# Four transformer blocks on one core: aside weight work packed into fewer pieces, output rounding ahead of its turns, one context group's norm on DVE

## The chip, the cores and the metric

The kernel runs on one core of a Trainium2 chip. The metric is the time of one execution on the device in microseconds (us); the times below are medians over runs, and one further execution was taken with the profiler on. The engines are called PE (matmul), PEld (its weight loads), DVE (vector), ACT (scalar), POOL (GpSimd) and SP (which issues most DMAs here).

## The reference

Four cross-attention blocks follow one another on x of 4 x 1024 x 288, with a context of 4 x 64 x 288 and 16 heads of 18. Blocks 0 and 3 are alike: self-attention, cross-attention and a feed-forward net, all with activations rounded to 8-bit levels per token and weights to 8-bit levels per output row:

```python
def quant_act(x):
    s = jnp.max(jnp.abs(x), axis=-1, keepdims=True) / 127.0 + 1e-08
    q = jnp.clip(_ste_round(x / s), -127.0, 127.0)
    return (q, s, jnp.sum(q, axis=-1, keepdims=True))
...
h = layer_norm(x, ln1_g, ln1_b, 1e-06)          # self-attention
q8, s, sm = quant_act(h)
q, k, v = (quant_linear(q8, s, sm, w, b) for w, b in ...)
a8, sa, sma = quant_act(attn(q, k, v))
x = x + quant_linear(a8, sa, sma, wo1, bo1)
h = layer_norm(x, ln2_g, ln2_b, 1e-05)          # cross-attention
q = quant_linear(*quant_act(h), wq2, bq2)
k, v = cond @ wk2.T + bk2, cond @ wv2.T + bv2
x = x + quant_linear(*quant_act(attn(q, k, v, mask)), wo2, bo2)
h = layer_norm(x, ln3_g, ln3_b, 1e-05)          # feed-forward
h = gelu(quant_linear(*quant_act(h), wfc1, bfc1))
return x + quant_linear(*quant_act(h), wfc2, bfc2)
```

Block 1 is an attention to two parts of the context, block 2 a fake-quantised self- and cross-attention with a gated feed-forward; the change touches no instruction of theirs except through `level_pieces`, which block 2 also draws on to prepare block 3's self-attention weights.

## The kernel before

x lies in SBUF as 32 tiles of 128 tokens x 288. `quant_net` runs blocks 0 and 3 in two stages.

**Self-attention (`quant_self`).** For each batch b of 4, head group g of 4 (four heads in one 128-row tile), half of the queries qh of 2 and key tile kt of 8 there is one step: four score matmuls (L2042), two exponentials on ACT (L2052), the four weighing matmuls of the step before (L1998), and then one call of `step()`. `weigh` copies its sum to `oT` on DVE after eight steps (L2009); one step later `turn_heads` transposes it (L1953) and divides by the row sums (L1959, L1960). `step()` hands out one piece of the work that lies beside: first from the list `side` in order, and only if `side` is empty from the generator `spare`. `side` holds `operands` (queries and keys of the next group, 4 pieces), `levels` (norm and rounding of the next batch, 12), `values` (8), `output` (rounding of the attention's result, its turns and the product with `wo` into x, 7 pieces per half batch) and, in the last batch, `early` (12: the norm and turn of the first context group). A piece ends at a `yield`.

`spare` is `ctx_aside` and then `ff_aside`: it checks the mask, makes levels of the weights `wq2`, `wo2`, `wfc1` and `wfc2` (`level_pieces`: a load, row extrema, rounding of 96 x 384 parts on DVE at L1605 to L1611, three transposes on PE at L1621, a copy at L1632 and, for the feed-forward, a store), and projects the context to keys (L1686, L1695, L1706, L1710) and values (L1731). `ctx_aside` has the tag `kv` with one buffer for masks, keys and values; POOL clears it ahead of each use (L1681, L1724). Several of its pieces hold nothing, or only a load or a memset. After the last step come `turn_heads()`, `run(spare)` (all that is left of `spare`) and what is left of `side`.

In `output`, one piece rounds a pair of tiles (`round_levels`, L1436 to L1444 on DVE); the next piece rounds the second pair and turns the first (`turn_levels`: transposes L1456, copy L1459).

**Context and feed-forward (`ctx_stage`, `ff_stage`, in block 0 also block 1's `vip_aside` and `vip_tokens`).** `run_stages` is a planner: generators yield the cost of each piece ("d" DVE, "a" ACT, "g" POOL, "p" PE) and the planner picks which one goes on. Context goes in groups of four tiles; the first (tiles 0 to 3) has been prepared by `early`, the others begin with the norm (`norm_apply`: ACT at L1423, then a product and a sum on POOL at L1426 and L1427), row maximum L1324, scale L1326, scaling L1333, turn L1350. Each group's head loop projects the queries (L2261, product with the scales L2269 on DVE), scores (L2277), exponentials (L2280), weighs (L2288, L2296), turns (L2304) and divides (L2307, L2308). POOL adds the bias of `wo` (L1784).

The instructions are written in this order, but the framework orders them again for each engine when the program is built, by what it takes to be ready.

Of the kernel before, what the change touches and what calls it, by code (L numbers as in the profile page):

```python
# [36 lines left out]
P = 128  # L37
# [4 lines left out]
HP = 32  # L42
# [9 lines left out]
EXP, GELU, SIDE = "exp", "gelu", "side"  # L52
CB = (C + N_TERMS) // NC3
# [1125 lines left out]
class Fast(Net):  # L1179
# [250 lines left out]
    def round_levels(self, h, tag):  # L1430


        nc = self.nc
        _, m, n = h.shape
        sc = self.sm.tile([P, m], F32, tag=f"sc{tag}", name="sc", bufs=10)
        nc.vector.tensor_reduce(sc, h, AX.X, ALU.max, apply_absolute_value=True)  # L1436
        nc.vector.tensor_scalar(sc, sc, 1.0 / 127.0, 1e-8, ALU.mult, ALU.add)
        rs = self.stat([P, m], f"rs{tag}")
        nc.vector.reciprocal(rs, sc)
        q = self.wk.tile([P, m, n], BF16, tag=f"q{tag}", name="q")  # L1440
        for j in range(m):
            t = h[:, j, :]
            nc.vector.tensor_scalar(t, t, rs[:, j : j + 1], MAGIC, ALU.mult, ALU.add)
            nc.vector.tensor_scalar(q[:, j, :], t, MAGIC, None, ALU.subtract)  # L1444
        return q, sc
# [100 lines left out]
    def level_pieces(self, np_, wd, n_in, width, p, put, sw, bias=None):  # L1546
# [24 lines left out]
        yield  # L1571
# [74 lines left out]
    def ctx_aside(self, w, ctxT, mask, cw, np_):  # L1646
# [8 lines left out]
        for b in range(B):  # L1655
            m = np_.tile([P, NTB * T], F32, tag="kv", name="msk")
            nc.sync.dma_start(
                m.rearrange("p (t k) -> p t k", k=T), mask[b].rearrange("(t p) k -> p t k", p=P)
            )
            yield  # L1660
            yield
            self.watch_range(0.0, 0.0, m, "mext")
# [10 lines left out]
        for g in range(NG):  # L1673
# [5 lines left out]
            kg = np_.tile([P, NTB * T], F32, tag="kv", name="kg")  # L1679
            kg = kg.rearrange("p (b k) -> p b k", b=B)  # L1680
            nc.gpsimd.memset(kg, 0.0)  # L1681
            yield
            yield
# [18 lines left out]
            for pr in range(2):  # L1702
# [10 lines left out]
                yield  # L1713
# [3 lines left out]
        wv = np_.tile([P, 1152], F32, tag="wn", name="wn", bufs=3)  # L1717
        wv = wv[:CK, : NC3 * C].rearrange("p (c o) -> p c o", c=NC3)
        nc.sync.dma_start(wv, w["wv2"].rearrange("(c p) o -> p c o", p=CK))
        yield  # L1720
        for b in range(B):
            vb = np_.tile([P, NTB * T], F32, tag="kv", name="vb")
            vb = vb.rearrange("p (j r d) -> p j r d", r=2, d=HP)
            nc.gpsimd.memset(vb, 0.0)  # L1724
            yield
# [71 lines left out]
    def quant_self(self, L, w, beside, ready, early):  # L1797
# [5 lines left out]
        with ExitStack() as es:  # L1803
# [126 lines left out]
            def output(b, hf):  # L1930
                a = state[b]["a"][hf]
                now = None
                for j in range(0, 4 + 2, 2):
                    ahead = None
                    if j < 4:
                        ahead = self.round_levels(a[:, j : j + 2, :], "o")
                    if now:
                        q, sc = now
                        aT = self.wk.tile([CK, NC3, 2 * P], BF16, tag="qTo", name="aT", bufs=1)
                        self.turn_levels(q, CK, aT)  # L1940
                    yield
                    if now:
                        for n in range(2):
                            t = b * NTB + hf * 4 + j - 2 + n
                            self.level_residual(aT, sc, wo, t, n, wo["b"])
                            yield
                    now = ahead
# [27 lines left out]

            def step(n=1):
                while side and n:
                    if next(side[0], side) is side:
                        side.pop(0)
                    else:  # L1980
                        n -= 1
                if n:
                    next(spare, None)
# [220 lines left out]
    def ctx_stage(self, cw, g2, b2, pool, nb, made):  # L2204
# [16 lines left out]
        def tokens(b, hf):  # L2221
# [8 lines left out]
            else:  # L2230
                h = self.wk.tile([P, 4, C], F32, tag="h", name="h", bufs=nb)
                for j in range(4):
                    self.norm_apply(h[:, j, :], t0 + j, stats[b], g2, b2)
                    if j % 2:
                        yield "a1.1&g3.2", 0 if j == 1 else None, SIDE
# [1374 lines left out]
```

## Time and profile before

| what | value |
|---|---|
| median of 3 runs | 4927.91 us (4926.48 to 4930.47) |
| profiled execution, whole | 4935.42 us |
| its span, first to last instruction | 4933.7 us |
| mean granted PE clock | 0.849 |
| busy: PE, DVE, ACT, POOL | 4260.1, 2997.3, 3071.3, 1273.6 us |
| last attention matmul (L1998) to first context matmul (L2261), block 0 | 806.2 to 830.1 us |
| the same, block 3 | 4483.0 to 4501.2 us |

Busy times are over the whole span and mix stages with different limits, so the work is read by stretches of time. A wait is listed as who waited for whom, with sum, number and longest in us. In a line of the timeline, the first number is the start in us from the first instruction, the second the duration, and the square bracket at the end says how long the engine sat idle before it and what ended that.

### The profile page before, as it was taken

What the parts mean: (1) busy time and instruction counts of PE and PEld (TensorE: products, weight loads), DVE (VectorE), ACT (ScalarE), POOL (GpSimd) and SP (SyncE); (2) the same over time, 40 slices, a digit from 0 to 9 for tenths busy, and PEclk for the clock granted to TensorE, in tenths of its full rate; (3) what the DMA queues carried; (4) which work ended last, traced back from release to release, by engine and by line L of the source; (5) the groups of instructions that cost most, each with busy time, mean ns of one, the idle gap of its engine ahead of it and who ended that gap; (6) DMA issues with size and microseconds to landing.
All of it is one profiled execution on the core that took longest, in us unless ns stands there. A gap on an engine that the chain in (4) does not pass through costs nothing. (4 is left out here: it accounts for less than half of the span.)

```text
span 4933.7 us, 63765 instructions
## 1 busy us (share of the span) xinstructions
PE 4260.1 (86%) x23291; PEld 1717.8 (35%) x23291; DVE 2997.3 (61%) x6691; ACT 3071.3 (62%) x4355; POOL 1273.6 (26%) x1910
## 2 busy tenths in 40 slices
PE   4999998878998979997888873899998999997776
PEld 2233323445565411110233331455443233322343
DVE  8454336755654589999787878333234444436775
ACT  3776675664753279998888853212114776675796
POOL 2001002543222476410112224111111000004664
PEclk9999998889999955555697875899998999998888
DMA  3000003100001221000000022001000000001000
GB/s 84 4 4 12 11 9 85 41 31 7 13 13 58 108 63 33 26 6 0 23 27 25 22 94 71 30 9 34 1 3 16 3 4 12 11 20 43 12 17 21
DMA packets 137701, 135.99 MB, mean 28 GB/s; under 512 B 69276, under 2 KB 114972, under 8 KB 135712
## 3 DMA queue, kind: packets, MB, share of 16 engines
q1 hardware_dynamic: 136176, 128.13, 8.7%
q0 software_dynamic: 1200, 3.69, 0.3%
q8 instruction: 185, 3.03, 0.3%
q14 instruction: 140, 1.15, 0.1%
HBM read 79.92 MB, written 43.47 MB: 25 GB/s over the span
## 5 line engine op out<-in xcount | busy, mean ns | idle before, releaser
L2052 ACT ACTIVATE e<-ps 128x1024 f32<-128x1024 f32 x1024 | 992.6, 1021 | 388.2 <-PE ps L2042 377.7
L2042 PE MATMUL ps<-qT,kT 32*128 32x512 f32 x4096 | 630.4, 647 | 5.8 <-DVE sext L1971 5.8
L3076 DVE TENSOR_REDUCE top<-e 128x2 f32<-128x2048 f32 x256 | 563.5, 2275 | 13.9 <-ACT e L3069 13.7
L1998 PE MATMUL ps<-e,v 128*32 128x512 f32 x4096 | 554.7, 613 | 5.2 <-DVE oT L2009 5.2
L3445 PE MATMUL ps<-qk 32*128 32x512 bf16 x1024 | 499.6, 604 | 40.7 <-ACT e L3069 38.9
L3494 ACT ACTIVATE e<-ps 128x1024 f32<-128x1024 f32 x512 | 484.4, 1054 | 79.4 <-PE ps L3485 60.8
L3069 ACT ACTIVATE e<-ps 128x1024 f32<-128x1024 f32 x512 | 520.1, 1152 | 6.7 <-PE ps L3445 3.3
L3497 DVE TENSOR_SCALAR eb<-e 128x2048 bf16<-128x2048 f32 x256 | 321.7, 1260 | 49.2 <-ACT e L3494 46.8
L1780 POOL TENSOR_TENSOR x<-x,y 128x288 f32<-128x288 f32 x192 | 152.7, 804 | 705.9 <-DVE y L1779 416.7
L3485 PE MATMUL ps<-qk,kz 64*128 64x512 bf16 x1024 | 230.1, 446 | 42.3 <-ACT e L3494 38.4
L2042 PEld LDWEIGHTS ps<-qT,kT 32*128 32x128 f32 x4096 | 189.7, 185 | 209.5 <-issue 123.3
L2512 PE MATMUL psf<-hT,w 128*128 128x512 f32 x576 | 257.9, 600 | 0.6 <-ACT hT L2504 0.6
L1426 POOL TENSOR_TENSOR h<-h,g 128x288 f32<-128x288 f32 x168 | 136.5, 814 | 434.1 <-ACT h L1423 424.5
L1998 PEld LDWEIGHTS ps<-e,v 128*32 128x32 f32 x4096 | 81.3, 108 | 399.3 <-issue 348.4
L3445 PEld LDWEIGHTS <-qk 32*128 32x128 bf16 x1024 | 53.1, 99 | 464.8 <-issue 463.9
L3394 ACT ACTIVATE gl<-psf,bf 128x512 f32<-128x512 f32 x72 | 46.0, 684 | 270.0 <-PE psf L2516 265.7
L1355 ACT COPY qT<-ps 128x640 bf16<-128x640 bf16 (+3 forms) x252 | 149.7, 640 | 81.3 <-PE ps L1350 81.1
L1897 POOL TENSOR_TENSOR v<-y,wv1b 128x288 f32<-128x288 f32 x64 | 51.5, 811 | 524.2 <-DVE y L1894 524.2
L3398 DVE SCALAR_TENSOR_TENSOR u<-psf,bf,gl 128x512 f32<-128x512 f32 x72 | 51.1, 746 | 213.6 <-ACT gl L3394 213.6
L1350 PE MATMUL ps<-idb,q 128*128 128x128 bf16 (+2 forms) x1128 | 108.0, 240 | 78.5 <-ACT q L1334 47.1
L277 PEld LDWEIGHTS <-qT 98*128 98x128 bf16 (+2 forms) x1344 | 134.2, 104 | 118.0 <-issue 48.2
L3069 ACT ACTIVATION_READ_ACCUMULATOR e<-ps 128x1 f32 x512 | 172.4, 337 | 0.0
(507 smaller groups left out, 7776.6 us busy)
## 6 DMA issues: line engine op xcount, KB each, us to landing
raw<-y SPq DMA_DIRECT2D x32, 432.0 KB
in<-raw SPq DMA_DIRECT2D x30, 432.0 KB
kz<-qk SPq DMA_DIRECT2D x128, 64.0 KB
wn<-in_L_wfc SPq DMA_DIRECT2D x12, 432.0 KB
x<-in_x SPq DMA_DIRECT2D x4, 1152.0 KB
vvo<-vt SPq DMA_DIRECT2D x16, 288.0 KB
vo<-vvo SPq DMA_DIRECT2D x4, 1152.0 KB
rawq<-y SPq DMA_DIRECT2D x32, 144.0 KB
```

Of the source, the lines that this page charges most:

```text
L1355: nc.scalar.copy(qT[:, c0 : c0 + r, j0 * P : (j0 + per) * P].rearrange("p c (a t) -> p a c t", a=per), ps[:width, : per * r * P].rearrange ...
L1780: nc.gpsimd.tensor_tensor(self.x[:, t, :], self.x[:, t, :], y, ALU.add)
L1998: nc.tensor.matmul(acc[i * HP : (i + 1) * HP, :], lhsT=st["v"][:, kt, h * (D + 1) : h * (D + 1) + HP], rhs=es_[i // 2][:, i % 2, :], start ...
L2042: nc.tensor.matmul(pss[i // 2][:, i % 2, :], lhsT=self.row_tile(kT, i)[:, kt * P : (kt + 1) * P], rhs=self.row_tile(qT, i)[:, qh * 512 : ( ...
L2052: nc.scalar.activation(e, ps, AF.Exp, scale=SCALE)
L2512: nc.tensor.matmul(o, lhsT=lhs(i)[:, c, :], rhs=rhs(i)[:, c, :], start=(c == 0), stop=False)
L3069: nc.scalar.activation(e[:, j, :].rearrange("p (a n) -> p a n", a=2), sc, AF.Exp, scale=rstep, accum_out=sums[:, t, h0 + j : h0 + j + 1],)
L3076: nc.vector.tensor_reduce(top[:, t, h0 : h0 + 2], e, AX.X, ALU.max)
L3445: self.last = self.nc.tensor.matmul(ps[:, c, :], lhsT=self.row_tile(qT, i)[:, g, qt * P : (qt + 1) * P], rhs=self.row_tile(kT, i)[:, g, c ...
L3485: nc.tensor.matmul(pss[i][:, n, :], lhsT=kz[rows, i, kt * P : (kt + 1) * P], rhs=qT[rows, g, qh * 512 : (qh + 1) * 512], start=True, stop= ...
L3494: nc.scalar.activation(e[:, 2 * n : 2 * n + 2, :], ps, AF.Exp, scale=step)
L3497: nc.vector.tensor_scalar(eb, e, MAGIC, MAGIC, ALU.add, ALU.subtract)
```

## The change

- `ctx_aside` yields less often. Pieces that held only a load, a memset or nothing are joined with others: masks, keys and values are fetched or cleared one or two pieces ahead, with two `kv` buffers in place of one, and the two halves of `kb` and the store of the keys become one piece. It has 33 pieces where it had 54.
- The first `yield` after a fetch gives the value IDLE. When the next piece of `spare` follows an IDLE, `step()` lets it go along with a piece of `side`.
- `output` rounds both pairs in its first two pieces, and turns and multiplies them in the six after. `round_levels` uses one tag `qr` for the levels of input and output, where each had its own.
- The norm of the second context group (tiles 4 to 7) is done by `norm_dve` (L1412, L1415, L1416, all on DVE), with the planner's cost "d2.4" per two tiles.

```diff
--- before.py
+++ after.py
@@ -50,6 +50,7 @@
 
 N_TERMS = 6
 EXP, GELU, SIDE = "exp", "gelu", "side"
+IDLE = "idle"
 CB = (C + N_TERMS) // NC3
 
 
@@ -1437,7 +1438,7 @@
         nc.vector.tensor_scalar(sc, sc, 1.0 / 127.0, 1e-8, ALU.mult, ALU.add)
         rs = self.stat([P, m], f"rs{tag}")
         nc.vector.reciprocal(rs, sc)
-        q = self.wk.tile([P, m, n], BF16, tag=f"q{tag}", name="q")
+        q = self.wk.tile([P, m, n], BF16, tag="qr", name="q")
         for j in range(m):
             t = h[:, j, :]
             nc.vector.tensor_scalar(t, t, rs[:, j : j + 1], MAGIC, ALU.mult, ALU.add)
@@ -1568,7 +1569,7 @@
             return m, wn
 
         loaded = [load(c0) for c0 in range(0, oc, per)[:2]]
-        yield
+        yield IDLE
         yield
         for c0 in range(0, oc, per):
             m, wn = loaded.pop(0)
@@ -1652,14 +1653,25 @@
         nc.sync.dma_start(bk, w["bk2"])
         bv = self.load_bc(np_, w["bv2"], C, "bv2")
         ctx = self.load_ctx(np_, ctxT)
-        for b in range(B):
-            m = np_.tile([P, NTB * T], F32, tag="kv", name="msk")
+
+        def kv(name):
+            return np_.tile([P, NTB * T], F32, tag="kv", name=name, bufs=2)
+
+        def mask_of(b):
+            m = kv("msk")
             nc.sync.dma_start(
                 m.rearrange("p (t k) -> p t k", k=T), mask[b].rearrange("(t p) k -> p t k", p=P)
             )
+            return m
+
+        ms = [mask_of(0), mask_of(1)]
+        yield IDLE
+        yield
+        for b in range(B):
+            self.watch_range(0.0, 0.0, ms[b], "mext")
+            if b + 2 < B:
+                ms.append(mask_of(b + 2))
             yield
-            yield
-            self.watch_range(0.0, 0.0, m, "mext")
         wq, wo = cw["wq"], cw["wo"]
         yield from self.level_pieces(
             np_, w["wq2p"], C, CK, P, lambda c: (wq["T"][:, :, c * P : (c + 1) * P], False),
@@ -1670,17 +1682,34 @@
         )
         nc.sync.dma_start(cw["swo"].rearrange("(c p) -> p c", p=CK), swo)
         kb = cw["kb"]
-        for g in range(NG):
+
+        def keys_of(g):
             wk = np_.tile([P, 1152], F32, tag="wn", name="wn", bufs=3)
             wk = wk[:CK, : NC3 * P].rearrange("p (c o) -> p c o", c=NC3)
             nc.sync.dma_start(
                 wk, w["wk2"].rearrange("(c p) o -> p c o", p=CK)[:, :, g * P : (g + 1) * P]
             )
-            kg = np_.tile([P, NTB * T], F32, tag="kv", name="kg")
-            kg = kg.rearrange("p (b k) -> p b k", b=B)
+            kg = kv("kg").rearrange("p (b k) -> p b k", b=B)
             nc.gpsimd.memset(kg, 0.0)
-            yield
-            yield
+            return wk, kg
+
+        def values_of(b):
+            vb = kv("vb").rearrange("p (j r d) -> p j r d", r=2, d=HP)
+            nc.gpsimd.memset(vb, 0.0)
+            return vb
+
+        ahead = keys_of(0)
+        yield IDLE
+        yield
+        for g in range(NG):
+            wk, kg = ahead
+            if g + 1 < NG:
+                ahead = keys_of(g + 1)
+            else:
+                wv = np_.tile([P, 1152], F32, tag="wn", name="wn", bufs=3)
+                wv = wv[:CK, : NC3 * C].rearrange("p (c o) -> p c o", c=NC3)
+                nc.sync.dma_start(wv, w["wv2"].rearrange("(c p) o -> p c o", p=CK))
+                ahead = values_of(0)
             ps = self.ps1()
             for k in range(NC3):
                 nc.tensor.matmul(
@@ -1710,19 +1739,13 @@
                 nc.vector.tensor_scalar(
                     kb[:, :, g, pr : pr + 1], ps[:, :B].unsqueeze(2), SCALE, None, ALU.mult
                 )
-                yield
             nc.vector.tensor_scalar(kg, kg, wq["sw"][:, g : g + 1], None, ALU.mult)
             nc.sync.dma_start(cw["kbd"][:, :, g, :], kg)
             yield
-        wv = np_.tile([P, 1152], F32, tag="wn", name="wn", bufs=3)
-        wv = wv[:CK, : NC3 * C].rearrange("p (c o) -> p c o", c=NC3)
-        nc.sync.dma_start(wv, w["wv2"].rearrange("(c p) o -> p c o", p=CK))
-        yield
         for b in range(B):
-            vb = np_.tile([P, NTB * T], F32, tag="kv", name="vb")
-            vb = vb.rearrange("p (j r d) -> p j r d", r=2, d=HP)
-            nc.gpsimd.memset(vb, 0.0)
-            yield
+            vb = ahead
+            if b + 1 < B:
+                ahead = values_of(b + 1)
             ps = self.ps1()
             self.mm(ps[:, :C], ctx[:, :, b].rearrange("p c r k -> p c (r k)"), wv, 0, C)
             for r in range(2):
@@ -1929,22 +1952,18 @@
 
             def output(b, hf):
                 a = state[b]["a"][hf]
-                now = None
-                for j in range(0, 4 + 2, 2):
-                    ahead = None
-                    if j < 4:
-                        ahead = self.round_levels(a[:, j : j + 2, :], "o")
-                    if now:
-                        q, sc = now
-                        aT = self.wk.tile([CK, NC3, 2 * P], BF16, tag="qTo", name="aT", bufs=1)
-                        self.turn_levels(q, CK, aT)
+                qs = []
+                for j in range(0, 4, 2):
+                    qs.append(self.round_levels(a[:, j : j + 2, :], "o"))
                     yield
-                    if now:
-                        for n in range(2):
-                            t = b * NTB + hf * 4 + j - 2 + n
-                            self.level_residual(aT, sc, wo, t, n, wo["b"])
-                            yield
-                    now = ahead
+                for j, (q, sc) in zip((0, 2), qs):
+                    aT = self.wk.tile([CK, NC3, 2 * P], BF16, tag="qTo", name="aT", bufs=1)
+                    self.turn_levels(q, CK, aT)
+                    yield
+                    for n in range(2):
+                        t = b * NTB + hf * 4 + j + n
+                        self.level_residual(aT, sc, wo, t, n, wo["b"])
+                        yield
 
             def heads_done(b, g, qh, o):
 
@@ -1973,14 +1992,21 @@
             state = {}
             side = []
 
+            rest = {"next": None}
+
+            def spare_piece():
+                rest["next"] = next(spare, None)
+
             def step(n=1):
                 while side and n:
                     if next(side[0], side) is side:
                         side.pop(0)
                     else:
                         n -= 1
+                        if rest["next"] == IDLE:
+                            spare_piece()
                 if n:
-                    next(spare, None)
+                    spare_piece()
 
             def run(gen):
                 for _ in gen:
@@ -2230,9 +2256,13 @@
             else:
                 h = self.wk.tile([P, 4, C], F32, tag="h", name="h", bufs=nb)
                 for j in range(4):
-                    self.norm_apply(h[:, j, :], t0 + j, stats[b], g2, b2)
+                    if t0 == 4:
+                        self.norm_dve(h[:, j, :], t0 + j, stats[b], t0 + j, g2, b2)
+                    else:
+                        self.norm_apply(h[:, j, :], t0 + j, stats[b], g2, b2)
                     if j % 2:
-                        yield "a1.1&g3.2", 0 if j == 1 else None, SIDE
+                        cost = "d2.4" if t0 == 4 else "a1.1&g3.2"
+                        yield cost, 0 if j == 1 else None, SIDE
                 hT, sc = yield from self.levels(h, None, CK, "x", 0, nb, SIDE)
                 srep = self.wk.tile([P, 512], F32, tag="srep", name="srep", bufs=nb)
                 for j in (0, 2):
```

## The prediction

> **What bounds the kernel now.** I read the stretches of blocks 0 and 3 first (busy time by stretch), then the waits of TensorE inside the two attentions, then the timeline where each attention hands over. Attention runs from 85 to 806 us in block 0 and from 3764 to 4483 us in block 3. By stretches:
>
> ```profile
> 3800.00:3900.00 100.00, 100.00 (x744) 30.19 (x736) 42.43 (x116) 78.61 (x86) 6.39 (x8) 1.00 0.01 3
> 4480.00:4500.00 20.00, 10.87 (x70) 5.58 (x63) 12.81 (x45) 4.71 (x8) 3.33 (x5) 0.68 0.22 53
> 4500.00:4600.00 100.00, 67.89 (x327) 29.59 (x324) 68.31 (x206) 57.76 (x102) 58.54 (x95) 0.81 0.11 34
> ```
>
> The columns are PE, PEld, DVE, ACT, POOL busy, then granted clock, DMA share, GB/s. Inside attention PE is full (100 of 100 us), so only PE work or PE waits count there. At the hand-over PE is half empty at clock 0.68, and in the context and feed-forward stage no engine is full: latency decides. The PE waits inside block 0's attention (from 85 to 806 us; sum, times, longest):
>
> ```profile
> PE ps L1456 <- DVE q L1444: 8.0, 4, 3.3
> PE ps L2042 <- DVE sext L1971: 3.0, 2, 2.0
> PE ps L1998 <- DVE oT L2009: 2.6, 1, 2.6
> ```
>
> Block 3 has 7.7, 2.8 and 2.6. The first line is `output`: the turn of a pair waits until that pair is rounded. The third lies at 585 us: DVE sat 2.5 us in the memset of L1732, which waited for POOL's memset of the single `kv` buffer (L1724), which waited for a store; oT queued behind it. The hand-over of block 3:
>
> ```profile
> 4488.76 0.66 DVE L1632 COPY to<-ps 128x288 bf16<-128x288 bf16 x2 [1.63 <-DMA w2d<-to]
> 4489.12 0.56 PEld L1621 LDWEIGHTS <-q 96*128 96x128 bf16 x6 [3.10 <-DVE to L1632]
> 4501.18 2.72 PE L2261 MATMUL ps<-hT,wq2T 96*128 96x512 bf16 x6 [0.68 <-DVE y L1777]
> 4509.90 1.35 DVE L1324 TENSOR_REDUCE amx<-h 128x4 f32<-128x1152 f32 x1 [5.27 <-POOL h L1427]
> 4511.76 5.61 DVE L1326 TENSOR_SCALAR sc<-amx 128x4 f32<-128x4 f32 x1
> 4523.47 2.08 PE L2277 MATMUL ps<-qcT,kbd 64*128 64x512 f32 x4 [8.84 <-DVE qcT L2269]
> ```
>
> See three things: left-over weight pieces (L1621, L1632) sit in the tail between the last attention matmul (4483.0) and the first context matmul (4501.2), 18.2 us; in block 0 the same gap is 806.2 to 830.1, 23.9 us. Then DVE waits for the second group's norm on POOL and is held again in a tiny scale, and PE waits 8.84 us for a product queued behind both.
>
> **What the Trainium skill says.** "SBUF — State Buffer", section "Who interferes with whom": a tensor_scalar of DVE can use the port pair shared with GpSimd and then blocks fully until the other is done. The trace fits: L1326 takes 5.61 us here against a median of 0.17, and POOL works nearly without gap until 4517.35. "Perfetto Trace Analysis", section "Tensor Engine Instruction (MATMUL, LD_WEIGHTS)": DVE, ACT and GpSimd are strict FIFOs; the 8.84 us fit. "TensorE: Matmul & The Clock Gate", section "What's actually happening": an idle window of about 3.4 us halves PE's clock. The trace fits: granted clock 0.50 from 4490 to 4507 and from 815 to 836.
>
> **The change, part by part.**
>
> Packing. I count turns from the code: 4 x 4 x 2 x 8 = 256 calls of `step` per block. Side pieces take 180 of them before; the spare generator has 54 + 31 = 85 pieces, gets 76, and 9 of `wfc2` are left for `run(spare)` (7 of them, 21 transposes, are seen in each tail). After: `ctx_aside` has 33, `ff_aside` 31, so 64; `output` has 8 pieces where it had 7, so side takes 186; one IDLE piece rides along. All 64 fit and 7 steps stay free. So the tail loses its weight work: in block 3 DVE 2.0 (L1611) + 2.0 (L1632) + 1.6 waiting for the store = 5.6; in block 0 3.3 + 1.9 = 5.2 and slower neighbours beside POOL's norms. Cross-check by the chain that stays in block 3: last weigh, oT 0.7, L1953 0.7, reciprocal and product 0.9, rounding both pairs 5, then twice turn 0.8, copy 0.8, two products 1.6: about 13 us against 18.2. I take **-6 and -5.5** (ends -2 to -10 and -2 to -8). What is late next is the output chain itself, and in block 0 the key-part copies L2550, queued on DVE (PE waits 4.3 us for them).
>
> The moved pieces cost PE their transposes. Two plain steps take 4.37 us (109.74 to 114.11), a step with one weight piece 2.31 (781.41 to 783.72): 0.13 more, x 9 = **+1.2 per block**. The merged key piece issues the matmuls of both `kb` halves with a DVE copy between, and `acc` holds one of two PSUM buffers; existing waits of that kind are 0.5 and 1.2 us, I take 0.5 x 4 = **+2** (0 to 5). One more residual falls into the tail (0.9 for its three matmuls at half clock): **+0.9**. Mask, key and value loads are issued two pieces ahead as before; SP gets the same DMAs, POOL the same memsets. With two `kv` buffers a memset waits for the store of two pieces earlier; a store lands in 2.6 us (605.99 to 608.59), two steps are 4.4, so the 2.6 us wait goes: **-2.5 per block** (0 to -5, as the other DVE waits on L1724, 3.2 at most, were mostly hidden).
>
> Rounding ahead. Both roundings are issued before the first turn, one step (2.2 us) earlier than now. Of 8.0 and 7.7 us of turn waits the longest, 3.3, leaves about 1; the others go: **-6 per block** (-3 to -7.8). The second rounding, 2.4 us (0.74 + 0.15 + 0.15 + 2 x 0.365 + 2 x 0.30 with gaps), now lies ahead of no PE work of its pair. The shared tag "qr" keeps two buffers; input and output rounding follow one another in the side list, so I cost it at nothing, covered by the turns between (0 to +1).
>
> Second group's norm. Removed: 4 ACT of 0.62 and 8 POOL of 0.8 = 6.4 us. Added: 4 x (0.42 + 0.45 + 0.45) = 5.3 us of DVE (L1412, L1415, L1416). In block 0 the POOL norms lie wholly beside the tail (808.5 to 816.2): **0** (-3 to +5). In block 3 the 5.27 and 5.61 us on DVE are what puts PE 8.84 us late; the third group keeps POOL, so not all goes: **-7** (-10 to +2). The planner gets "d2.4" for the norm; following `run_stages` through both versions, only the first 40 or so hand-outs of each stage change, with group 2 ahead of group 1; the rest keeps its order.
>
> Sum: tails -11.5, turns -12, memset waits -5, costs 2 x (1.2 + 2 + 0.9) = +8.2, norm -7: **-27.3**. The profiled execution took 4935.4 (span 4933.7 and 1.7 around it), 7.5 over the median; so 4908.1 on its scale, and **4900.6** on the median's.
>
> **The rivals.**
> A, DVE becomes the tail's bound: the norm's 5.3 us take the place of the removed 5.2 to 5.6. For: DVE is busy 13.6 of 15 us from 815 to 830. Against: much of that is locks beside POOL, and in block 3 only 7.6 of 11. Then tails and norm give nothing: -8.8, 4919.
> B, slower: group 2 goes first on DVE. Its norm 5.3, maximum 1.35 and four scalings 1.5 stand ahead of the first group's products (L2269), and one lock like the 5.61 comes on top: 13.8 per block, with the tails' gain swallowed: -8.8 + 27.6 = +18.8, 4946.7. For: the hand-out order. Against: group 2's inputs are ready, so its norm can fill gaps. It decides from 4.4 us of delay per block on.
> C, it doesn't do what it says: instructions are reordered when the program is built (two of nine left-over pieces were already drawn forward), so packing and early rounding may come out as they were: norm -7, memset -5, costs +8: 4924.
>
> **How the numbers follow.** Forecast 0.62 (4880 to 4916: its terms at their ends), A 0.16, B 0.12, C 0.10. 0.2%, about what a measurement of this kernel can tell from no change, is 9.9 us. Faster takes the forecast and half of A: 0.70; same half of A and most of C: 0.16; slower B and a rest of C: 0.14. The range 4878 to 4936 reaches over A and C and leaves out most of B.
>
> **What would show it.** No L1621 or L1632 after the last L1998 of either block; last L1998 to first L2261 near 13 us in block 3 and 18 in block 0; PE's wait on L1444 inside attention under 3 us per block; in block 3 no DVE wait on L1427 ahead of the first group's last L2269, and PE's wait there under 3 us. The sum is wrong if attention itself gets longer (new waits at L1706 or L1998), or if the first group's reduction (L1324, now 49.5 us after the last L1998 in both blocks) comes later.

## The result: 13 us slower, and the profile after

The changed kernel takes 4941.02 us (median of 9 runs, 4936.76 to 4944.83) against 4927.91 beside it; the ratio is 1.0026, 95% interval 1.0016 to 1.0036. The forecast was 4900.6 us, faster. Its profiled execution (span 4936.6 us) lies 2.7 us under its median, the one before 7.5 over: the two spans differ by only 2.9 us, so I compare stretches within them.

Line numbers of the kernel after are a little higher: L1998 is now L2024 (weighing), L2042 L2068 (scores), L2261 L2291 (context queries), L2269 L2299, L2277 L2307, L2407 L2437 (scale columns), L1777 L1800 (`y`), L1706 and L1710 L1735 and L1739 (`kb`), L1444 and L1456 L1445 and L1457, L1621 and L1632 L1622 and L1633, L1324 L1325, L1326 L1327, L1412 L1413. Busy time by stretch (PE, PEld, DVE, ACT, POOL, then granted clock, DMA share, GB/s), kernel after:

```profile
3800.00:3900.00 100.00, 100.00 (x744) 30.24 (x744) 34.63 (x91) 78.59 (x86) 6.38 (x8) 1.00 0.01 3
4480.00:4500.00 20.00, 13.27 (x103) 4.28 (x95) 12.11 (x30) 11.21 (x14) 8.91 (x11) 0.89 0.08 27
4500.00:4600.00 100.00, 73.87 (x328) 31.80 (x329) 65.39 (x204) 50.76 (x89) 49.13 (x82) 0.75 0.11 34
```

Undisturbed attention is as before (100 of 100 us, 744 matmuls). In this execution it ends at 4491.3, 8.3 us later than before, so the second line still holds 11 us of it. The waits of PE in block 0 (86 to 813 us; sum, times, longest), kernel after:

```profile
PE ps L278 <- DVE y L1800: 4.3, 4, 2.0
PE ps L1735 <- DVE kb L1739: 3.8, 2, 2.6
...
PE ps L2024 <- DVE oT L2035: 2.6, 2, 1.8
...
PE ps L1457 <- DVE y L1800: 1.4, 2, 0.7
```

The 8.0 us on the rounded pair (before L1444, now L1445) are gone. In their place stand 5.7 us on `y` and 3.8 us on `kb`; oT still costs 2.6. Block 3's hand-over, kernel after:

```profile
4499.50 0.56 PE L1457 MATMUL ps<-idb,q 128*96 128x128 bf16 x3 [6.41 <-DVE q L1445]
4507.92 2.72 PE L2291 MATMUL ps<-hT,wq2T 96*128 96x512 bf16 x6 [0.68 <-DVE y L1800]
4511.77 2.08 PE L2307 MATMUL ps<-qcT,kbd 64*128 64x512 f32 x4 [1.14 <-DVE qcT L2299]
4512.61 2.59 DVE L1325 TENSOR_REDUCE amx<-h 128x4 f32<-128x1152 f32 x2
4515.13 0.42 DVE L1327 TENSOR_SCALAR sc<-amx 128x4 f32<-128x4 f32 x1
```

This part did much of what was forecast: no L1622 or L1633 follows the last L2024, L1325 no longer waits for POOL, L1327 takes 0.42 us where L1326 took 5.61, and PE's 8.84 us became 1.14. Yet the whole is slower. Four lengths per block show where it went (us; last weigh end is the end of the last L1998 or L2024; "first reduction" is the first group's row maximum after its head loops; "stage" runs from there to the end in block 3, and in block 0 to block 2's projection in `product4`, L2516 before and L2546 after, so that it holds block 1 too):

| block, kernel | attention | to first context matmul | to first reduction | stage |
|---|---|---|---|---|
| 0 before | 720.9 | 23.8 | 49.4 | 779.0 |
| 0 after | 727.0 | 12.2 | 50.6 | 780.5 |
| 3 before | 719.0 | 18.1 | 49.3 | 450.6 |
| 3 after | 725.3 | 16.6 | 44.5 | 445.3 |

Attention is 6 us longer in each block, and block 0's gain of 11.6 us at the first context matmul is lost before the first group's reduction. Block 2, which the change leaves alone, took 2178.8 us before and 2172.5 after, so a single span can't tell less than about 6 us. The verdicts below therefore use the ratio to the kernel before, timed beside each run, with us worked out as (ratio - 1) x 4928.

### The profile page after: what moved, and what is told of

Its sections match the earlier page's. It is cut to its first block, busy times and chain, and to the rows that moved or that the text cites. A ratio compares the mean times of both kernels' runs of the same rounds, so it can differ in the third digit from the quotient of the medians.

```text
span 4936.6 us, 63761 instructions
## 1 busy us (share of the span) xinstructions
PE 4264.7 (86%) x23291; PEld 1718.2 (35%) x23291; DVE 3004.1 (61%) x6715; ACT 3066.8 (62%) x4347; POOL 1263.5 (26%) x1894
## 5 line engine op out<-in xcount | busy, mean ns | idle before, releaser
L2068 PE MATMUL ps<-qT,kT 32*128 32x512 f32 x4096 | 634.2, 648 | 1.5 <-DVE a L1979 1.5
L2024 PE MATMUL ps<-e,v 128*32 128x512 f32 x4096 | 557.1, 615 | 5.1 <-DVE oT L2035 5.1
L2068 PEld LDWEIGHTS ps<-qT,kT 32*128 32x128 f32 x4096 | 186.6, 185 | 200.9 <-issue 127.8
L2024 PEld LDWEIGHTS ps<-e,v 128*32 128x32 f32 x4096 | 81.4, 108 | 401.1 <-issue 347.4
L2035 DVE COPY oT<-ps 128x512 f32<-128x512 f32 x64 | 44.2, 691 | 249.9 <-PE ps L2024 249.6
```

The source lines that it names most:

```text
L2024: nc.tensor.matmul(acc[i * HP : (i + 1) * HP, :], lhsT=st["v"][:, kt, h * (D + 1) : h * (D + 1) + HP], rhs=es_[i // 2][:, i % 2, :], start ...
L2068: nc.tensor.matmul(pss[i // 2][:, i % 2, :], lhsT=self.row_tile(kT, i)[:, kt * P : (kt + 1) * P], rhs=self.row_tile(qT, i)[:, qh * 512 : ( ...
```

## The experiments

Each run stands against the kernel before on the same chip. Attention and stage are for blocks 0 / 3, from its profile.

| run | ratio (95%) | us | attention | stage |
|---|---|---|---|---|
| after | 1.0026 (1.0016 to 1.0036) | +12.8 | 727.0 / 725.3 | 780.5 / 445.3 |
| e1 early rounding | 1.0012 (1.0006 to 1.0019) | +5.9 | 711.2 / 712.1 | 787.2 / 466.6 |
| e2 packing | 1.0036 (1.0024 to 1.0049) | +17.7 | 739.2 / 740.2 | 770.3 / 439.2 |
| e3 norm on DVE, d2.4 | 1.0042 (1.0027 to 1.0057) | +20.7 | 720.2 / 719.0 | 792.2 / 457.8 |
| e4 after, kb halves apart | 1.0001 (0.9994 to 1.0009) | +0.5 | 720.8 / 718.8 | 781.9 / 450.5 |
| e5 after, old norm | 0.9974 (0.9963 to 0.9984) | -12.8 | 726.5 / 723.8 | 766.0 / 437.9 |
| e6 e4 and e5 | 0.9959 (0.9945 to 0.9973) | -20.2 | 719.7 / 716.8 | 772.3 / 442.5 |
| e7 norm on DVE, old cost | 1.0008 (0.9999 to 1.0016) | +3.9 | 721.3 / 717.7 | 778.2 / 447.4 |
| e8 d2.4 alone | 1.0038 (1.0024 to 1.0051) | +18.7 | 721.5 / 717.9 | 785.3 / 457.9 |
| e9 after, old cost | 0.9970 (0.9959 to 0.9982) | -14.8 | 730.0 / 724.6 | 769.5 / 436.5 |
| e10 e9, kb halves apart | 0.9945 (0.9932 to 0.9958) | -27.1 | 720.1 / 715.9 | 768.9 / 442.1 |
| e11 e2, kb halves apart | 0.9965 (0.9954 to 0.9977) | -17.2 | 722.0 / 720.3 | 766.5 / 439.4 |
| e12 shared tag alone | 1.0020 (1.0009 to 1.0032) | +9.9 | 732.4 / 724.6 | 778.5 / 450.5 |
| e13 e1, own tags | 0.9976 (0.9968 to 0.9984) | -11.8 | 705.2 / 701.7 | 783.8 / 463.8 |
| e14 after, three qr | 1.0054 (1.0040 to 1.0067) | +26.6 | 744.1 / 735.9 | 777.5 / 445.0 |
| e15 e10, three qr | 0.9994 (0.9985 to 1.0004) | -3.0 | 730.0 / 725.6 | 772.2 / 438.0 |
| e16 after, own tags | 1.0044 (1.0032 to 1.0056) | +21.7 | 727.7 / 728.3 | 778.8 / 447.1 |
| e17 e10, own tags | 0.9958 (0.9945 to 0.9971) | -20.7 | 713.2 / 715.7 | 770.1 / 439.4 |
| e18 e10, own tags, one for input | 0.9915 (0.9902 to 0.9928) | -41.9 | 711.3 / 705.5 | 772.5 / 440.5 |

### One part at a time: e1, e2, e3

e1 is the kernel before with the new `output` and the shared tag; e2 has the packed `ctx_aside`, IDLE and the shared tag, with the old `output`; e3 has only the norm of group 2 on DVE with its cost d2.4.

> Before with the early output rounding and its shared tag alone; the aside pieces and the norm stay as before. Theory 1 (attention is where the change loses, the packed pieces and the early rounding share it): turn waits fall from 8.0 us per block to under 1, but new waits of the second product on y take their place (5.7 us seen after), so attention stays within 3 us of before per block; tail still with 7 left-over pieces or more (output needs 8 pieces, so 1 or 2 more pieces are left per attention end); time +2 to +8 us. Rival 1 (early rounding is sound and only packing loses): attention 5 us shorter per block, time -5 to -12 us.

> Before with the packed aside pieces (two kv buffers, IDLE pieces, shared rounding tag) alone; output in its old form, norm on POOL. Theory 1: the merged key piece brings PE waits of 3.8 us on kb and a stretch at half clock, some +6 us of attention per block, less what the turn's congestion at the end gives; hand-over 8 to 12 us shorter in block 0, 3 in block 3; time -5 to +6. Rival 1 (packing alone loses): +10 us or more. Rival 2 (the forecast's sum for packing): -15 us.

> Before with the second group's norm on DVE and its planner cost alone. Theory 1: attention exactly as before; block 3 from the last weighing matmul to the end 3 to 6 us shorter, block 0's stage 0 to 3 us longer; time -5 to 0. Rival (the group that goes first on DVE delays the first one, as the forecast's rival B): +10 us or more, all of it between the last weighing matmul and the first group's reduction.

Each part, cut out like this, makes the kernel slower. e1 shortens attention by 7 to 10 us, but its eighth piece per half batch takes places from `spare`: more weight pieces are left for the tail (29 weight transposes are recorded there, 19 before), and the stage grows by 8.2 and 16.0 us. e2 is the mirror image: stages 8.7 and 11.4 us shorter, attention 18.3 and 21.2 longer. e3 leaves attention alone and lengthens both stages. So none of my terms could be read off one part alone, and two things were to be split further: what in e3 costs, and what in e2. Packing and early rounding do gain, as e11 and e13 show below, once the merged key piece or the shared tag is taken out of them.

### The norm: DVE's time or the order? e5, e7, e8, e9

e5 is the kernel after with the old norm and cost. e7 is e3 with the old cost; e8 has only the cost; e9 is the kernel after with the old cost. The edits of e7 and e9, and then of e8:

```diff
-                        cost = "d2.4" if t0 == 4 else "a1.1&g3.2"
+                        cost = "a1.1&g3.2"
```

```diff
-                        yield "a1.1&g3.2", 0 if j == 1 else None, SIDE
+                        cost = "d2.4" if t0 == 4 else "a1.1&g3.2"
+                        yield cost, 0 if j == 1 else None, SIDE
```

> The changed kernel with the second group's norm back on ACT and POOL at its old planner cost. Theory 2 (formed from the first four runs: the norm on DVE makes the first context group later, wherever it is put): attention as in the changed kernel (727 and 725 us), from the last weighing matmul on 7 to 15 us shorter over both blocks; time -8 to +3 against before. Rival (in the changed kernel the norm only fills DVE gaps that packing left, and the 20 us it cost alone came from the left-over pieces beside it): from the last weighing matmul on within 3 us of the changed kernel, time +9 to +15.

> Before with the second group's norm on DVE, but handed to the planner at its old cost, so that the order of the hand-outs is that of before. If the 20 us of the norm come from the order (group 2's levels handed out ahead of the first group's loop): within 4 us of before. If they come from DVE's own time (5.3 us in the way of the first group's products): +10 to +20.

> Before with only the planner's cost of the second group's norm changed to d2.4; the norm itself stays on ACT and POOL. If the order does it: +10 to +25, with the first group's reduction 8 to 12 us later in block 0. If DVE's time does it: within 4 us of before.

> The kernel after the change with the norm of the second group still on DVE, but the planner told the old cost a1.1&g3.2. Order theory: the hand-out order that d2.4 brings is what costs, the norm's own place next to nothing. Then this run is the sum of packing with early rounding (-13.0 us, e5) and of the norm with the old cost (+3.9, e7): -9 us against before, from -15 to -3, that is about 22 us under the kernel after the change; the first group's row maximum comes 41 to 47 us after the last weighing, as in e5 and e7, and the stage of block 3 lies under 445. Rival, DVE's time: the 5.3 us of norm stand in the way of the first group wherever the planner puts them; then +8 to +13 us against before, as after the change.

This is the clearest answer of the study. A norm that still runs on ACT and POOL, with nothing but another figure for the planner (e8), costs 18.7 us; the norm really on DVE with the old figure (e7) costs 3.9, and its interval holds zero; that is 16.8 less than in e3. And in the changed kernel the old figure alone takes it from +12.8 to -14.8. It is the hand-out order that costs; the norm's own place on DVE costs at most a few us in sum. (It isn't free where it stands. In block 3 of e7 the norm takes about 11 us of DVE instead of 5.3, with products and sums of 1.04 us each where I took 0.45, and PE waits 7.24 us at 4508.42 for the first product behind it. That takes the place of the 8.84 us that PE waited later before.) How the order costs is seen on PE where the first group's fourth query projection stands. The timeline of PE before:

```profile
840.29 0.82 PE L2261 MATMUL ps<-hT,wq2T 96*128 96x512 bf16 x3
...
852.93 0.71 PE L2407 MATMUL ps<-idf,scol 128*128 128x128 f32 x4
```

and of e8 (L2262 and L2408 are the same instructions):

```profile
838.80 0.71 PE L2408 MATMUL ps<-idf,scol 128*128 128x128 f32 x4
841.85 0.72 PE L2408 MATMUL ps<-idf,scol 128*128 128x128 f32 x2 [2.33 <-POOL scol L2396]
...
846.23 0.82 PE L2262 MATMUL ps<-hT,wq2T 96*128 96x512 bf16 x3
```

Before, the first group's fourth projection runs at 840.29 and the second group's scale columns come 12.6 us later. With d2.4 the scale columns stand ahead of that projection in PE's queue; PE waits 2.33 us for POOL to write them, and the projection comes at 846.23. The first group's reduction follows 4.4 us later after the last weighing in block 0 (53.8 against 49.4) and 7.7 us in block 3 (57.0), and the stages are 6.3 and 7.3 us longer. The kernel after has the scale columns ahead of the fourth projection too (timeline of PE, then of DVE):

```profile
847.51 1.22 PE L2437 MATMUL ps<-idf,scol 128*128 128x128 f32 x4
...
852.97 1.14 PE L2291 MATMUL ps<-hT,wq2T 96*128 96x512 bf16 x3
```

```profile
832.26 0.68 DVE L2299 TENSOR_TENSOR qcT<-ps,srep 128x512 f32<-128x512 f32 x1
832.87 1.34 DVE L1325 TENSOR_REDUCE amx<-h 128x4 f32<-128x1152 f32 x1
...
836.38 2.95 DVE L1334 TENSOR_SCALAR h<-h,rsx 128x288 f32<-128x288 f32 x4
...
839.82 0.69 DVE L2299 TENSOR_TENSOR qcT<-ps,srep 128x512 f32<-128x512 f32 x1
...
845.61 0.69 DVE L2299 TENSOR_TENSOR qcT<-ps,srep 128x512 f32<-128x512 f32 x1 [1.71 <-PE ps L2291]
854.15 0.69 DVE L2299 TENSOR_TENSOR qcT<-ps,srep 128x512 f32<-128x512 f32 x1 [7.85 <-PE ps L2291]
```

The four products of the first group start over 22 us. In the first 7.6 of them the second group's maximum and scalings (L1325, L1334) stand on DVE between the first product and the second; in the last 8.5 DVE waits for PE, with the scale columns ahead of the fourth projection. In e9 the four start within 9 us, and the scale columns come after (timelines of DVE and PE):

```profile
835.56 1.27 DVE L2299 TENSOR_TENSOR qcT<-ps,srep 128x512 f32<-128x512 f32 x2
...
844.49 0.69 DVE L2299 TENSOR_TENSOR qcT<-ps,srep 128x512 f32<-128x512 f32 x1
```

```profile
840.64 0.81 PE L2291 MATMUL ps<-hT,wq2T 96*128 96x512 bf16 x3 [0.25 <-DVE qcT L2299]
...
851.20 0.71 PE L2437 MATMUL ps<-idf,scol 128*128 128x128 f32 x4
```

The first reduction then comes 38.4 and 37.6 us after the last weighing instead of 50.6 and 44.5, and the stages are 11.0 and 8.8 us shorter: 19.8 of the 27.6 us between the two ratios. The rest is no more than the two intervals and the scatter of single spans leave open.

### The merged key piece: e4, e6, e10, e11

One line, put after the scaling of each half of `kb` (L1739):

```diff
                     kb[:, :, g, pr : pr + 1], ps[:, :B].unsqueeze(2), SCALE, None, ALU.mult
                 )
+                yield
```

e4 is the kernel after with it; e6 is e5 with it; e10 is e9 with it and e11 is e2 with it.

> The changed kernel with one more yield after each half of kb (as before the change; 72 pieces in place of 64, 7 free steps at the end take nearly all). Theory 1: PE waits on kb fall from 3.8 to about 2 us per block, the half-clock stretch at 310 us goes, attention 4 to 6 us shorter per block than in the changed kernel; time against before +0 to +4 us. Rival (the merged piece is harmless, the waits on y do it): within 2 us of the changed kernel, +11 to +15.

> The same with the kb halves apart again: packing, early rounding, no norm on DVE, no merged key piece. Theory 2: attention 720 us per block as in the run with the split halves, stages as in the run before this one in the list: -12 to -22 us against before. Rival (the norm is harmless beside packing): as the run with the split halves, -2 to +4.

> The fastest version so far (e6: packed with the two kb halves as two pieces, early rounding, norm on ACT and POOL) with the norm of the second group on DVE and the old planner cost. Order theory: e6 (-20.2 us against before) plus what e7 showed for the norm (+3.9): -16 us, from -23 to -10; so no better than e6. Rival: with POOL freed of eight products and sums, block 3's hand-over gains the 5 to 7 us once forecast, and the run beats e6: -25 to -30.

> The kernel before with the packed aside work and the shared tag, but with the two kb halves as two pieces; output and norm as before. In e2 (the halves merged) attention was 18 and 21 us longer. Theory 1: the merged piece costs 6 us per block, as between the kernel after and e4, and the rest comes from the old output beside full spare slots: attention 12 to 15 us longer than before, stages 8 to 11 shorter, +2 to +10 us in all. Theory 2: the merged piece is nearly all of it: attention at most 6 us longer, and the run is 5 to 12 us faster than before.

From after to e4 and from e9 to e10 the ratio falls by 0.0025 both times: 12.3 us, some 6 us per block. From e5 to e6 it is 7.4 us. Attention is 6.2 to 9.9 us shorter in these three pairs; part of it is given back in most stages, as 72 pieces don't all fit and a few weight transposes are back in the tail (4 recorded, none in after, e5 and e9). Of e11 theory 2 held, more strongly than it said: beside the old `output` the merged piece had cost 17 and 20 us of attention. The price shows in the timeline of the kernel after. In the first merged piece of block 0 the second half of a `kb` waits for the copy of the first:

```profile
308.76 0.17 DVE L1391 TENSOR_SCALAR ve<-mv 128x8 f32<-128x8 f32 x1
...
311.20 0.17 DVE L1406 SCALAR_TENSOR_TENSOR nmr<-mv,rstd 128x8 f32<-128x8 f32 x1
311.28 0.16 DVE L1739 TENSOR_SCALAR kb<-ps 128x4 f32<-128x4 f32 x1
311.49 1.86 PE L1735 MATMUL ps<-csm,kg 64*128 64x1 f32 x8 [2.64 <-DVE kb L1739]
```

The copy of 0.16 us stands in DVE's queue behind the next batch's norm statistics, of which the last 13 operations, of 0.17 us each, start a fifth of a us apart. PE is idle for 2.64 us, and from 310.9 to 317.7 its granted clock is 0.50. But the wait isn't what it takes. The second merged piece has none; PE is busy throughout, and its clock is halved all the same (timeline of PE, then by stretch):

```profile
396.15 1.05 PE L1735 MATMUL ps<-csm,kg 64*128 64x1 f32 x8
397.13 1.12 PE L2068 MATMUL ps<-qT,kT 32*128 32x512 f32 x2
398.18 1.05 PE L1735 MATMUL ps<-csm,kg 64*128 64x1 f32 x8
```

```profile
399.70:403.10 3.40, 3.40 (x15) 0.70 (x10) 0.12 (x1) 1.94 (x2) 0.53 (x1) 0.50 0.27 82
```

A merged piece has sixteen matmuls that are one column wide, with two score matmuls between the halves. In the six kernels that have it (after, e2, e5, e9, e14, e16) half clock begins within 4.4 us of the start of 46 of the 48 such pieces, among them 22 of the 24 in which PE didn't wait. With the halves apart, eight score and eight weighing matmuls stand between them: after none of the 56 key projections in before, e1, e3, e7, e8, e12 and e13 did the clock fall. In e4 and e10 it did after six of the seven with a wait of 1.6 us and after none of the nine without. By stretches, kernel after:

```profile
300.00:330.00 30.00, 25.39 (x152) 9.23 (x150) 16.57 (x50) 13.21 (x14) 2.11 (x3) 0.89 0.07 20
400.00:450.00 50.00, 46.97 (x239) 18.19 (x240) 26.24 (x83) 19.67 (x21) 4.93 (x16) 0.80 0.13 39
```

and e4:

```profile
300.00:330.00 30.00, 26.41 (x180) 8.04 (x180) 15.68 (x47) 17.13 (x19) 2.11 (x3) 0.94 0.03 10
400.00:450.00 50.00, 44.56 (x301) 15.81 (x297) 28.94 (x93) 29.08 (x31) 3.91 (x14) 0.93 0.11 29
```

Busy time hardly differs (72.4 against 71.0 us), but the clock does: 30 x 0.11 + 50 x 0.20 = 13.3 us are lost to it after, 30 x 0.06 + 50 x 0.07 = 5.3 in e4, and 391 matmuls run in these 80 us against 481. Elsewhere e4 loses more. Over the whole attention, (1 - clock) x length comes to 18.8 and 17.1 us after (blocks 0 and 3) and to 13.7 and 11.9 in e4: 5.1 and 5.2 of the 6.2 and 6.5 us of attention. From e9 to e10 it is 10.2 and 6.9 of 9.9 and 8.7. PE's waits would not have shown it: in block 0 they are nearly the same for `kb` in both (3.8 and 3.4 us). In e10 against e6 the norm sits on DVE instead of ACT and POOL, at -27.1 against -20.2; their intervals overlap, so a gain from it is not shown.

### The shared tag: e12 to e18

A tag names a set of buffers that tiles of one kind take in turn. e12 has nothing but the tag. e13 is e1 with the old tags. e14 and e15 give `qr` a third buffer in the kernel after and in e10. e16 and e17 have two tags of two buffers each in the kernel after and in e10; for this to fit in SBUF, the tag `to` has one buffer. e18 is e10 with two tags, one buffer for the input. The one line in its versions (the comments name the runs), and the second edit of e16 and e17:

```diff
-        q = self.wk.tile([P, m, n], BF16, tag=f"q{tag}", name="q")
+        q = self.wk.tile([P, m, n], BF16, tag="qr", name="q")                       # e12
+        q = self.wk.tile([P, m, n], BF16, tag="qr", name="q", bufs=3)               # e14, e15
+        q = self.wk.tile([P, m, n], BF16, tag=f"q{tag}", name="q")                  # e13, e16, e17
+        q = self.wk.tile([P, m, n], BF16, tag=f"q{tag}", name="q",
+                         bufs=1 if tag == "i" else 2)                               # e18
...
-                        to = np_.tile([P, run * P], BF16, tag="to", name="to", bufs=2)
+                        to = np_.tile([P, run * P], BF16, tag="to", name="to", bufs=1)
```

> The kernel before with nothing changed but the shared tag qr for the levels of input and output. Forecast step: covered by the turns between, 0 to +1 us per block; so -3 to +4 us in all, attention within 2 us of before. Rival: the input's rounding must wait until an output's pair has been turned, and the DVE queue behind it (oT, y, kb) comes late; then attention is 4 to 8 us longer per block and the run 8 to 16 us slower, and the packing alone (e2) was charged with it.

> The kernel before with early rounding of output, but with separate tags for the levels of input and output, two buffers each (e1 had the shared tag: +6 us, attention 7 to 10 us shorter than before). If the shared tag costs here what it cost alone (+10 us, e12), then attention is 10 to 15 us shorter than before and the run -2 to -8 us. If early rounding hides the tag, attention is as in e1 within 2 us and the run +4 to +8 us.

> The kernel after the change with a third buffer for qr, nothing else. If the tag costs inside the change what it cost alone: attention 4 to 6 us shorter per block than after the change, the run +1 to +5 us against before in place of +13. If early rounding hides it: attention within 2 us of after, the run +10 to +15 us.

> The fastest version so far (e10: -27 us) with a third buffer for qr. If the tag costs: -33 to -38 us. If it is hidden: -25 to -29 us. A rival that ends worse: with a third buffer DVE takes the next batch's norm and rounding earlier, ahead of oT and y, and attention is 3 to 8 us longer: -12 to -22 us.

> The kernel after the change with separate tags for the levels of input and output (two buffers each); to make room, the tag to of the weight transposes' copies has one buffer in place of two. If the shared tag is part of the loss: PE's waits on y (4.3 and 1.4 us in block 0's attention after the change) go, attention is 6 to 10 us shorter per block than after the change, and the run is -8 to +2 us against before in place of +13. If the tag costs nothing inside the change: attention within 2 us of after, +10 to +15 us. If the one buffer of to holds DVE up behind a store: waits on L1633 of 5 us and more, and up to +20 us.

> The fastest version so far (e10: -27 us; packing with the kb halves as two pieces, early rounding, norm of the second group on DVE at the old planner cost) with separate tags and one buffer of to. If the tag costs 5 to 8 us per block here too: -37 to -43 us. If not: -24 to -30 us. If the one buffer of to holds DVE up: -10 to -20 us.

> The version of e10 with separate tags, one buffer for the input's levels and two for the output's. If sharing is what puts the input's rounding ahead of y: y waits gone, -30 to -40 us. If DVE's order follows from the number of buffers, as with the third buffer in e15: the input's second rounding waits for the turn of the first, attention 3 to 8 us longer, -10 to -20 us.

The tag alone costs 9.9 us (e12): PE's idle time inside attention grows by 7.2 and 7.6 us. (Attention in e12's block 0 is longer by 11.5, but some 5 of that isn't the tag's: in this execution the score matmuls have half-clock durations from the start to 105 us, in the profile of before only from 90.6 to 100.8.) Beside early rounding, taking the tag back gains 17.7 (e1 to e13). The order of instructions on PE is the same in both of these pairs; on DVE it isn't. Timeline of e1, where the tag is shared:

```profile
300.12 0.75 DVE L1436 TENSOR_REDUCE sc<-h 128x2 f32<-128x576 f32 x1
...
301.31 0.65 DVE L1443 TENSOR_SCALAR h<-h,rsi 128x288 f32<-128x288 f32 x2
301.87 0.51 DVE L1777 SCALAR_TENSOR_TENSOR y<-ps,sc,wo1sw 128x288 f32<-128x288 f32 x1
302.44 0.53 PE L277 MATMUL ps<-wo1T,aT 96*128 96x288 bf16 x3 [1.96 <-DVE y L1777]
```

The norm and rounding of the next batch's input lie directly ahead of `y`, and PE's next product waits 1.96 us for it. With own tags (e13) no wait on this `y` is left in the attention's list. The same 4.3 us on `y` of the output product stand in the lists of e1, e4, e6, e10 and the kernel after; they are gone in e17 and e18. From e10 to e18 it is 14.8 us, with attention 8.8 and 10.4 us shorter: e18 has three buffers as e15 has, so it is the sharing and not their number. Of e14 neither theory held, and of e15 the worse rival, more than in full: with a third buffer the norm of the next input comes earlier in DVE's order, waits on `y` rise to 8.7 us in e14, and attention is 17.1 and 10.6 us longer than in the kernel after.

e16 doesn't give a clean answer for the changed kernel. Its waits on `y` went, but attention stayed, with one new wait of 6.3 us in block 0 and one of 6.5 in block 3 (L2068 on the quotient L1979). That wait is the price of the single `to` buffer, the third case of its expectation: ahead of the quotient DVE sits 5.40 and 5.65 us before the copy L1633, until a store has emptied the buffer. Without it attention would be some 5.6 and 3.5 us shorter than after, an estimate from these waits that no run shows. The single buffer also reaches into block 2, which prepares weights through `level_pieces`: that block took 2186.8 us in e16 and 2187.2 in e17, against 2172 to 2179 in all other profiles. So some 10 us of both runs are the price of that edit there, and in e16 the two new waits come on top. The tag probably costs inside the changed kernel too, but that isn't shown.

e18 is the fastest version: 4897.72 us (5 runs) against 4942.15 beside it, ratio 0.9915.

## Why the prediction was wrong

By its own terms, forecast total -27.3, measured +12.8:

- **"Only the first 40 or so hand-outs change"**: this is the step that failed. I had seen the changed order, and carried it at nothing in the forecast. It costs 27.6 us in the changed kernel (after to e9) and 18.7 alone (e8), and by itself turns the sign: with the old cost figure the change gives -14.8. Rival B had the place, the sign and part of the mechanism: it named the hand-out order, and the second group's maximum and scalings do stand on DVE ahead of the first group's second product. But it priced the norm on DVE with a lock, and e8 pays 18.7 with no norm there; the columns ahead of the fourth projection on PE it did not have. That its 27.6 for both blocks is also the difference from after to e9 is chance.
- **The merged key piece**, costed at +2 per block (0 to 5): 6 (4 from e5 to e6). I took the wait alone from existing rows of 0.5 and 1.2 us. A wait was up to 2.64, but the price is the half clock that followed 46 of 48 such pieces, with a wait or without. My reading that inside attention "only PE work or PE waits count" left the clock out, though the kernel before already loses 13.7 us to it in each attention, and though I had cited the Trainium skill, "TensorE: Matmul & The Clock Gate", section "What's actually happening", for the hand-overs. It says the clock is set over windows of about 3.4 us. The trace agrees inside attention too: at 310 and 410 us, 10 us slices have clock 0.66, which is two such windows at half (1 - 0.5 x 6.8 / 10).
- **The shared tag**, at nothing: +9.9 alone, 17.7 beside early rounding alone, 14.8 in the fastest version. "Covered by the turns between" looked at when a buffer is free; what moved was the order on DVE, and `y` came late. Inside the changed kernel its share stays open (e16).
- **Turn waits**, -6 per block: they went, and alone with own tags the early rounding shortens attention by 15.7 and 17.3 us (e13), more than twice my term. Part of that is weight work pushed into the tail, whose stages are 4.8 and 13.2 us longer; that e13 as a whole gains 11.8, near the 12 of my term, is a sum of the two and confirms nothing. In the changed kernel waits on `y` and `kb` took the place of the turn waits.
- **Tails**, -6 and -5.5: the first context matmul comes 11.6 and 1.5 us earlier after the last weighing, 13.1 in sum where 11.5 was forecast, but split otherwise. e5 has stages 13.0 and 12.7 shorter, more than forecast; there the first context matmul comes 7.0 us earlier and 2.4 later, and the gain shows at the first reduction, 8.8 and 10.9 earlier. In block 3 the gap is 16.6, not 13: PE waits 6.41 us for the rounding, which lies behind `y` and a norm of the second group on DVE (busy 8.69 of 10 us from 4490).
- **Norm on DVE**, 0 and -7: in the kernel after the waits of DVE and PE at the hand-over went as described, but e7 is +3.9 (-0.5 to +7.9). In e7 PE's wait of 8.84 us came back earlier, as 7.24 us behind the norm, and block 3's stage gained 3.2 us (447.4 against 450.6), which a single span can't tell from nothing.
- **Memset wait**, -2.5 per block: no gain seen. The wait at 585 us behind a memset is gone from PE's list, but two others on oT make up 2.6 us again; the longer, 1.76 us at 423.31, stands behind a weight's row maximum (L1581) that had waited 1.18 us for its load.

Two corrections, +27.6 for the order and 12.3 - 4 = 8.3 for the key piece, bring -27.3 to +8.6, 4.2 us from the measured value and inside its interval (7.9 to 17.7). That they add up is no proof that the rest was right: early rounding was worth more than forecast, the tag cost where nothing was put down, and e2 and e11 show that these parts don't add. That the sum comes so near is luck in part.

Of the signs that I had named for being wrong one came clearly: attention longer, with a new wait at L1706 (now L1735). The other, a later first reduction, came only in block 0 and by less than a single span can tell (50.6 against 49.4); in block 3 it came earlier (44.5 against 49.3).

## What to carry to other kernels

A planner's cost figure is a change of order, and is to be costed as one: look up which instruction now stands ahead of the first group's next one, on DVE and on PE. When a tile tag, a buffer count or a yield is touched, compare the order on the engine that fills the tile before counting waits. Where a small copy gates PE, ask what is queued ahead of it. And where PE is full, add up its granted clock as well as its waits: here sixteen one-column matmuls close together cost more through the clock than through any wait.

## What was not expected of the hardware

Sixteen matmuls one column wide (64x1, 8 in 1.05 us), with only two score matmuls between the halves, were followed by half clock 46 times of 48, and 22 times of 24 where PE had no idle wait at all. With the 2.64 us wait in the first such piece, the clock was 0.66 from 310 to 320 us, and 36 matmuls ran in that slice where undisturbed attention has 74.

Idle waits alone did not decide it. A wait of 2.61 us for `oT` between ordinary matmuls was followed by a clock of 0.57 over 4 us in the kernel before (at 585), and the same wait of 2.61 us by 1.00 in e12 (at 598).
